# Order of scores, values and exponentials in a causal attention loop, and the PSUM bank that holds the value sums

## The chip, the cores and the metric

The kernel runs on 1 core of a Trainium2 chip. The time is device microseconds of one execution. TensorE (PE) multiplies and transposes into PSUM, which has 8 banks of 128 partitions x 512 fp32; VectorE (DVE) and ScalarE (ACT) read PSUM and write SBUF; GpSimd (POOL) works on SBUF alone here; SyncE (SP) issues the DMAs. Each engine runs its own instructions in the order in which they were issued and waits at an instruction until what it needs is there.

## What is computed

One encoder-decoder layer in fp32. Encoder: 2 sequences of 77 tokens, D = 512, 16 heads of 32, self attention with a relative bias, feed-forward of 2048. Decoder: 2 sequences of 2048 tokens: causal self attention with a relative bias, cross attention to the encoder's output, feed-forward. What this change touches is the decoder's causal self attention:

```
def _mha(xq, xkv, w_in, b_in, w_out, b_out, bias):
    wq, wk, wv = jnp.split(w_in, 3, axis=0)
    ...
    scores = jnp.einsum('bhqd,bhkd->bhqk', q, k) / jnp.sqrt(jnp.asarray(hd, xq.dtype))
    scores = scores + bias[None]
    attn = jax.nn.softmax(scores, axis=-1)
    out = jnp.einsum('bhqk,bhkd->bhqd', attn, v)
    out = out.transpose(0, 2, 1, 3).reshape(Bq, Tq, D)
    return out @ w_out.T + b_out
...
sb = _rel_bias(dec_rel_self, Tt, Tt) + causal[None]
yn = _ln(y, dec_n1_s, dec_n1_b)
y = y + _mha(yn, yn, dec_sa_in_w, dec_sa_in_b, dec_sa_out_w, dec_sa_out_b, sb)
```

## The kernel before

**Tiling.** The 2048 queries of a batch b (0, 1) are four blocks m (0 to 3) of 512, each four tiles t (0 to 3) of 128. The 16 heads are four groups g of four heads r. A *unit* is one (b, m, g, t): 128 queries, four heads; there are 128. It sees i + 1 = 4m + t + 1 blocks of 128 keys: 1 to 4 in block 0, 5 to 8 in block 1, 9 to 12 in block 2, 13 to 16 in block 3. `pieces` cuts these into pieces of at most four key blocks: 9 is 4 + 3 + 2, 10 is 4 + 4 + 2, 11 is 4 + 4 + 3, 12 is 4 + 4 + 4, 16 four times 4.

**Steps of a unit.** `scores` (one call for each piece): four matmuls, one for each head, with 32 rows of the array each, into four banks (L374); DVE copies each head's bank to the buffer `pp` and keeps its maximum (L383; the last two key blocks go with the bias through L390); after the last piece L399 makes the negative maximum `nm`, and the four exponentials (L404, ACT, one for each head, over the whole width of the unit) are put into the list `late_exps`. `exps(k)` issues the first k of them. `turn`: transposes the probabilities of up to two pieces, one bank for each key block with its four heads (a *load*, L424), and copies each bank to `pts`, the first half of the loads on ACT (L430), the rest on DVE (L428). `values`: for each key block four matmuls, 32 columns of the array each, add v times the transposed probabilities into bank 7 (L441), which gathers the four units t of a group in its four quarters; after the last one the whole bank is copied to `oT` (L447). Later the sums of the exponentials divide `oT` on POOL (L469), and `out_job` (L251) projects it and adds the residual, which `residual` loads on SP and adds to the bias on POOL (L266).

**Two buffers.** `pp` holds the scores of two units, so while unit n is turned, unit n + 1 is complete or nearly so, and `may_score` lets a piece of unit n + 2 in as soon as unit n's turn has read that part.

**The main loop** takes the pieces two at a time. Each round is a *visit*: all exponentials still missing for this unit, `turn` (in block 0 another order of loads), at the unit's last visit `slot(n + 1)` (the *jobs* of that unit: projections of q, k and v, the output projection, norms, weight sums), a score piece, one or two exponentials, `values`, further score pieces. Within `turn` one exponential is issued behind the fourth load (or the last, if there are fewer) and one behind the last load. A unit of block 1 is one visit, of blocks 2 and 3 two.

**Banks.** `bank()` hands out banks 0 to 6 in turn (`count`), bank 7 is for the value sums. PE waits before it writes a bank until the engine that read it last is done. Behind the attention loop the feed-forward half takes over with banks 0 to 3 for `bank()`.

The lines of the main loop that are moved:

```
            if may_score():
                score_next()
            if ends:
                for f in behind[n + 1]:
                    f()
            exps((0, 2, 1, 1)[units[n][1]])
            for p in pair:
                values(*p)
            while may_score() and (len(pair) > 1 or units[n][1] == 0):
                score_next()
```

## Time and profile before

| what | value |
|---|---|
| median of 3 runs | 2781.49 us (2779.92 to 2781.69) |
| the profiled execution's own time | 2781.64 us |
| its span | 2779.9 us |
| granted PE clock | 0.998 |
| ACT and DVE busy | 1436.6 and 1888.2 us |
| HBM traffic | 129 GB/s over the span |

The attention loop, with the encoder and the first block's cross attention woven in, is the first 1705 us; its blocks begin at 29, 165, 381 and 616 us (batch 0) and 888, 1024, 1215 and 1448 us (batch 1). Then comes cross attention and feed-forward. A row of the timeline is: start, length, engine, line, operation, what it writes and reads, shape, number of records, and in brackets the engine's idle time before it and what ended it. A score matmul or a values matmul leaves two records in the trace, a transpose one: "x32" at L424 is eight loads, "x8" at L374 a piece (four heads), "x64" at L441 the values of eight key blocks. PEld are the weight loads, which run beside PE.

### The profile page before, as it was taken

How to read it: one execution, taken by the hardware profiler on the slowest of the kernel's cores; microseconds unless marked ns; L12 is line 12 of the kernel's file. 1: busy time of each engine (PE TensorE's matmuls, PEld its weight loads, DVE VectorE, ACT ScalarE, POOL GpSimd, SP SyncE). 2: the span in 40 equal slices, each digit the busy share in tenths (PEclk: the TensorE clock that was granted, in tenths of full speed). 3: DMA queues.
4: the chain of work that ended last, by engine and by line, in shares of the span. 5: the costliest groups of instructions: out<-in, count | busy, mean ns of one | idle time of the engine just before them, and what ended most of it. 6: DMA issues, size and time to landing. Idle time of an engine off the chain costs nothing. (4 is left out here: it accounts for less than half of the span.)

```text
span 2779.9 us, 66840 instructions
## 1 busy us (share of the span) xinstructions
PE 2750.5 (99%) x26294; PEld 2130.5 (77%) x26294; DVE 1888.2 (68%) x5420; ACT 1436.6 (52%) x2753; POOL 915.8 (33%) x777
## 2 busy tenths in 40 slices
PE   9999999999999999999999999999999999999998
PEld 5577776677666566676677667898989898989898
DVE  5776587788887578687788885555555646464645
ACT  3444466656666556666656665444444444444431
POOL 1501134400100412212200002364646474646456
PEclk9999999999999999999999999999999999999999
DMA  8433345411112521233211014574757565646465
GB/s 224 141 102 111 102 124 166 128 55 47 35 52 62 139 74 55 89 100 104 96 55 40 25 32 141 186 233 156 228 159 234 176 223 163 222 161 224 147 225 182
DMA packets 282251, 362.45 MB, mean 130 GB/s; under 512 B 39072, under 2 KB 156624, under 8 KB 281810
## 3 DMA queue, kind: packets, MB, share of 16 engines
q1 hardware_dynamic: 281938, 358.18, 41.0%
q8 instruction: 208, 3.41, 0.5%
q14 instruction: 105, 0.86, 0.1%
HBM read 314.49 MB, written 43.59 MB: 129 GB/s over the span
## 5 line engine op out<-in xcount | busy, mean ns | idle before, releaser
L404 ACT ACTIVATE pp<-pp,nm 128x128 f32<-128x128 f32 (+15 forms) x512 | 612.1, 1203 | 146.6 <-DVE nm L399 142.1
L383 DVE TENSOR_SCALAR_CACHE_REDUCE pp<-psum 128x512 f32<-128x512 f32 (+3 forms) x1024 | 559.3, 591 | 59.4 <-PE psum L374 57.7
L424 PEld LDWEIGHTS psum<-ident,pp 128*128 128x128 f32 x4352 | 473.1, 141 | 112.8 <-DVE pp L383 56.0
L424 PE MATMUL psum<-ident,pp 128*128 128x128 f32 x4352 | 535.8, 277 | 10.1 <-DVE mx L390 3.3
L430 ACT COPY pts<-psum 128x512 f32<-128x512 f32 (+3 forms) x592 | 300.6, 576 | 470.4 <-PE psum L424 339.0
L428 DVE COPY pts<-psum 128x512 f32<-128x512 f32 (+2 forms) x544 | 330.0, 660 | 66.2 <-PE psum L424 65.7
L374 PE MATMUL psum<-kT,q 32*128 32x512 f32 (+3 forms) x2560 | 357.0, 574 | 4.5 <-ACT nT L310 2.1
L441 PEld LDWEIGHTS psum<-pts,vv 128*32 128x32 f32 x8704 | 225.6, 110 | 123.3 <-issue 115.5
L1524 PE MATMUL psum<-pp 128*128 128x128 f32 x2560 | 304.5, 276 | 1.9 <-POOL pp L936 1.6
L1524 PEld LDWEIGHTS psum<-pp 128*128 128x128 f32 x2560 | 296.3, 192 | 8.6 <-issue 2.8
L441 PE MATMUL psum<-pts,vv 128*32 128x128 f32 x8704 | 278.2, 275 | 0.7 <-ACT pts L430 0.5
L936 POOL TENSOR_TENSOR pp<-pp 128x512 f32<-128x512 f32 x159 | 212.7, 1354 | 126.3 <-DMA pp<-in_dec_ff_wT_dram 66.3
L1495 PE MATMUL psum<-vv,pp 128*128 128x256 f32 x1024 | 236.2, 381 | 0.0
L374 PEld LDWEIGHTS psum<-kT,q 32*128 32x128 f32 x2560 | 121.3, 183 | 123.2 <-issue 80.2
L1495 PEld LDWEIGHTS psum<-vv,pp 128*128 128x128 f32 x1024 | 190.3, 190 | 25.8 <-issue 0.5
L390 DVE CUSTOM_DVE_ANT_0 pp<-psum,bias 128x256 f32<-128x256 f32 (+1 forms) x512 | 196.3, 412 | 14.7 <-PE psum L374 14.5
L1508 DVE TENSOR_TENSOR kT<-kT,psum 128x512 f32<-128x512 f32 x96 | 65.8, 686 | 191.1 <-PE psum L1495 190.9
L266 POOL TENSOR_TENSOR xr<-xr,row_dec_sa_out_b 128x512 f32<-128x512 f32 x30 | 38.2, 1276 | 417.9 <-DMA xr<-in_x_dram 313.1
L1495 PE MATMUL psum<-nT,pp 128*128 128x256 f32 x768 | 174.1, 380 | 0.0
L1511 ACT ACTIVATE kT<-kT,vecs 128x256 f32<-128x256 f32 x192 | 87.0, 501 | 156.7 <-DVE kT L1508 156.0
L1495 PEld LDWEIGHTS psum<-nT,pp 128*128 128x128 f32 x768 | 144.2, 190 | 20.3 <-issue 1.6
L469 POOL TENSOR_TENSOR oT<-rirows,oT 128x512 f32<-128x512 f32 x30 | 38.3, 1275 | 364.4 <-DMA rirows<-rec 327.9
(242 smaller groups left out, 3882.8 us busy)
## 6 DMA issues: line engine op xcount, KB each, us to landing
pp<-w_d SPq DMA_DIRECT2D x520, 256.0 KB
pp<-in_dec_ff_wT_dram SPq DMA_DIRECT2D x112, 256.0 KB
wqk<-in_dec_sa_in_wT_dram SPq DMA_DIRECT2D x76, 256.0 KB
bias<-tzg SPq DMA_DIRECT2D x128, 128.0 KB
pp<-wo_d SPq DMA_DIRECT2D x56, 256.0 KB
vv<-in_enc_ff_wT_dram SPq DMA_DIRECT2D x8, 1024.0 KB
xr<-in_x_dram SPq DMA_DIRECT2D x32, 256.0 KB
vv<-y SPq DMA_DIRECT2D x32, 256.0 KB
```

The lines of the kernel that those rows point to most:

```text
L374: nc.tensor.matmul(banks[r][:, : kn * P], q[rows4(r), ts(t, P)], kT[rows4(r), g, k0 * P : (k0 + kn) * P], start=True, stop=True,)
L383: nc.vector.tensor_scalar(p[:, k0 : k0 + far], s[:, :far], 1.0, None, ALU.mult, ALU.max, accum_out=st["mx"][:, r, c : c + 1],)
L390: nc.vector.tensor_tensor_reduce(p[:, k0 + far : i + 1], s[:, far:kn], near[:, 2 - (kn - far) :], 1.0, LOWEST, ALU.add, ALU.max, accum_out ...
L404: nc.scalar.activation(p, p, AF.Exp, bias=nm, accum_out=to)
L424: nc.tensor.transpose(pt[:, ts(x, P)], state[n]["p"][r][:, k], ident)
L428: nc.vector.tensor_copy(pts[:, : len(load), :], pt[:, :w])
L430: nc.scalar.copy(pts[:, : len(load), :], pt[:, :w])
L441: nc.tensor.matmul(ot[rows4(r), t, :], vv[:, k, ts(g * HC + r, HD)], got.pop((n, k, r)), start=(k == 0), stop=(k == i),)
L936: engine.tensor_tensor(out, a, b, ALU.subtract)
L1495: nc.tensor.matmul(mm[:, ts(f, TOK)], a[:, c, ts(f, P)], b[:, c, :], start=fresh and f == 0 and c == 0, stop=c == 1, skip_group_check=True,)
L1511: nc.scalar.activation(dst[:, e, :], src[:, e, :], AF.Relu, bias=vec("dec_ff1_b", f + e))
L1524: nc.tensor.matmul(psum[:, bank_i, ts(col, P)], lhs[:, c, :], w[:, c, :], start=fresh and k in (0, 3) and c == 0, stop=c == 3, skip_group_ ...
```

## The change

1. `bank()` takes the bank that has been handed out longest ago from a ring of all eight. `values` takes the oldest bank out of the ring and puts it back, as the newest, behind the copy of its sums.
2. `values` is called once for a visit's pair. In block 0 one bank gathers a group's four units as before and is copied whole on ACT. In the other blocks each visit has a bank of its own: the first visit's sums are copied to `oT` on ACT (128x128), the second visit's are added to them on DVE. In the first tile of the third group the sums stay in the bank over both visits (so `oT` is written after its last reader).
3. In blocks 1 to 3, a visit with two pieces scores up to two pieces ahead of `values`; what may still be scored comes behind as before.
4. The one or two exponentials behind `turn` are issued ahead of the score calls. In a turn of eight loads the exponential that was behind the fourth load is behind the eighth; in block 3 the one that followed the turn is left to the next place.
5. In a turn of eight loads (blocks 1 to 3) DVE copies loads 4 and 6 (counted from 0), ACT the other six.
6. The output projection of blocks 0 to 2 is one unit earlier, with its residual.

In the built program PE has the same instructions before and after, in another order. ACT's copies of whole banks to `pts` go from 544 to 688, DVE's from 496 to 352; ACT's copies of 128x128 to `oT` from 56 to 152; DVE's 24 copies of whole banks to `oT` are gone, its additions of 128x128 to `oT` go from 56 to 116 (56 of each of these two belong to the feed-forward half).

```diff
@@ -174,13 +174,13 @@
         oT_all = ac.tile([P, 6, TB * P], F32, name="oT")
         bo = ac.tile([P, D], F32, name="row_dec_sa_out_b")
         psum = ps.tile([P, 8, 512], F32, name="psum")
-        count = {"bank": 0, "banks": 7, "pts": 0, "oT": 0, "mm": 0}
+        count = {"pts": 0, "oT": 0, "mm": 0}
+        ring = list(range(8))
 
         def bank():
 
-            i = count["bank"] % count["banks"]
-            count["bank"] += 1
-            return psum[:, i, :]
+            ring.append(ring.pop(0))
+            return psum[:, ring[-1], :]
 
         def in_turn(what, tile):
             i = count[what] % tile.shape[1]
@@ -424,27 +424,47 @@
                     nc.tensor.transpose(pt[:, ts(x, P)], state[n]["p"][r][:, k], ident)
                     got[n, k, r] = pts[:, x, :]
                 w = len(load) * P
-                if o % 2 if first else o >= (len(loads) + 1) // 2:
+                if o % 2 if first else o in (4, 6) if len(loads) == 8 else o >= (len(loads) + 1) // 2:
                     nc.vector.tensor_copy(pts[:, : len(load), :], pt[:, :w])
                 else:
                     nc.scalar.copy(pts[:, : len(load), :], pt[:, :w])
-                if not first and o == min(3, len(loads) - 1):
+                if not first and o == (7 if len(loads) == 8 else min(3, len(loads) - 1)):
                     exps(1)
-            exps(HC if first else 1)
-
-        def values(n, k0, kn):
+            exps(HC if first else 0 if units[pieces[0][0]][1] == NMB - 1 else 1)
+
+        sums_held = {}
+
+        def values(pair):
+            n, k0, _ = pair[0]
             b, m, g, t = units[n]
             i = m * TB + t
-            for k in range(k0, k0 + kn):
-                ot = psum[:, 7, :].rearrange("p (t q) -> p t q", q=P)
+            k1 = pair[-1][1] + pair[-1][2]
+            whole = m == 0
+            key = (b, m, g) if whole else n
+            begun = key in sums_held
+            if not begun:
+                sums_held[key] = ring.pop(0)
+            v = sums_held[key]
+            ot = psum[:, v, ts(t, P)] if whole else psum[:, v, :P]
+            keep = t < TB - 1 if whole else (g, t) == (2, 0) and k1 <= i
+            for k in range(k0, k1):
                 for r in range(HC):
                     nc.tensor.matmul(
-                        ot[rows4(r), t, :], vv[:, k, ts(g * HC + r, HD)], got.pop((n, k, r)),
-                        start=(k == 0), stop=(k == i),
+                        ot[rows4(r)], vv[:, k, ts(g * HC + r, HD)], got.pop((n, k, r)),
+                        start=k == k0 and (whole or not begun), stop=k == k1 - 1 and (whole or not keep),
                     )
-                if t == TB - 1 and k == i:
-                    o = ots[b, m, g] = in_turn("oT", oT_all)
-                    (nc.vector.tensor_copy if m else nc.scalar.copy)(o, psum[:, 7, :])
+            if keep:
+                return
+            if (b, m, g) not in ots:
+                ots[b, m, g] = in_turn("oT", oT_all)
+            o = ots[b, m, g]
+            if whole:
+                nc.scalar.copy(o, psum[:, v, :])
+            elif k0 == 0 or begun:
+                nc.scalar.copy(o[:, ts(t, P)], ot)
+            else:
+                nc.vector.tensor_tensor(o[:, ts(t, P)], ot, o[:, ts(t, P)], ALU.add)
+            ring.append(sums_held.pop(key))
 
         ri_of = [const.tile([P, RB], F32, name=f"ri{i}") for i in range(2)]
         for t in ri_of:
@@ -1094,9 +1114,10 @@
                 jobs[NU + 5].append(fold_job())
             for t in range(TB):
                 end = x == len(blocks) - 1
-                jobs[u + NU + (2 if end else 7) + t].append(out_job(b, m, t))
+                out_at = u + NU + (2 if end else 7 if m == NMB - 1 else 6) + t
+                jobs[out_at].append(out_job(b, m, t))
                 if not end:
-                    light[u + NU + 6 + t].append(lambda b=b, m=m, t=t: residual(b, m, t))
+                    (light if x else late)[out_at - 1].append(lambda b=b, m=m, t=t: residual(b, m, t))
                 elif t < 2:
                     light[u + NU - 1].append(lambda b=b, m=m, t=t: residual(b, m, t))
                 if x:
@@ -1743,14 +1764,14 @@
             turned_to[n] = pair[-1][1] + pair[-1][2]
             if ends and n + 1 < end:
                 slot(n + 1)
-            if may_score():
-                score_next()
+            exps((0, 2, 1, 1)[units[n][1]])
+            for _ in range(2 if len(pair) > 1 and units[n][1] else 1):
+                if may_score():
+                    score_next()
             if ends:
                 for f in behind[n + 1]:
                     f()
-            exps((0, 2, 1, 1)[units[n][1]])
-            for p in pair:
-                values(*p)
+            values(pair)
             while may_score() and (len(pair) > 1 or units[n][1] == 0):
                 score_next()
             i += len(pair)
@@ -1759,7 +1780,8 @@
         for t in (2, 3):
             residual_load(*blocks[-1], t, pts_all[:, 2 * t - 3, :])
         late_loads()
-        count.update(bank=0, banks=4)
+        assert len(ring) == 8
+        ring[:] = range(4)
         side = cross(1)
         slot(end)
         for s in range(4):
```

## The prediction

> **What bounds the kernel now.** I read the page's busy table first.
>
> ```profile
> span 2779.9 us, 66840 instructions
> PE 2750.5 (99%) x26294; PEld 2130.5 (77%) x26294; DVE 1888.2 (68%) x5420; ACT 1436.6 (52%) x2753; POOL 915.8 (33%) x777
> ```
>
> PE bounds it, but matmuls are pipelined, so a waiting PE still shows as busy. What PE really needs is read from the start of one group to the start of the next, in the timeline of a visit where nothing waits (here the first visit of a unit of block 3, batch 0):
>
> ```profile
> 739.26 3.71 PE L424 MATMUL psum<-ident,pp 128*128 128x128 f32 x32
> 739.95 2.06 ACT L430 COPY pts<-psum 128x512 f32<-128x512 f32 x4 [4.48 <-PE psum L424]
> 742.90 1.14 PE L374 MATMUL psum<-kT,q 32*128 32x512 f32 x8
> 743.97 1.95 PE L441 MATMUL psum<-pts,vv 128*32 128x128 f32 x64
> 744.10 0.68 DVE L383 TENSOR_SCALAR_CACHE_REDUCE pp<-psum 128x512 f32<-128x512 f32 x1
> 745.86 1.14 PE L374 MATMUL psum<-kT,q 32*128 32x512 f32 x8
> 746.93 3.77 PE L424 MATMUL psum<-ident,pp 128*128 128x128 f32 x32
> ```
>
> Eight loads of transposes take 742.90 - 739.26 = 3.64 us, a score piece of four blocks 1.07, the values 1.89, the second piece 1.07: 7.67 in all. A group's busy time is its share plus a tail of 0.07 (1.14 against 1.07, 3.71 against 3.64). Next, the groups by shape, to see how much of PE's time is waiting:
>
> ```profile
> L424 PE MATMUL psum<-ident,pp 128*128 128x128 f32 x4352 | 535.8, 277 | 10.1 <-DVE mx L390 3.3 <-ACT pp L404 2.8 <-ACT nT L310 1.4
> L374 PE MATMUL psum<-kT,q 32*128 32x512 f32 x1600 | 255.4, 637 | 0.0
> L374 PE MATMUL psum<-kT,q 32*128 32x384 f32 x448 | 52.8, 533 | 0.0
> L374 PE MATMUL psum<-kT,q 32*128 32x256 f32 x448 | 45.3, 423 | 1.7 <-DVE pp L383 1.4 <-DVE kT L1043 0.3
> ```
>
> A score piece is 8 records, so 200, 56 and 56 pieces; clean they are busy 1.14, 0.93 (row at 454.83 below) and, taking the same step of 0.21 per block, 0.71 us: 228 + 52 + 40 = 320. The rows say 353.5, so some 33 us are waits for banks and about 2 more are idle. Transposes: 136 times 3.71 is 505; 192 turns instead of 136 full ones add about 56 x 0.15 = 8 of starts and tails; the row says 535.8, so 23 are waits, and 10 more idle. PE therefore waits about 70 us at these two lines in a chain that is otherwise matmul after matmul. That is the room. It is not spread evenly; by block of batch 0 (blocks 1, 2, 3) the scores take
>
> ```profile
> 165.00:381.20 216.20, 37.04 (x273) 13.16 (x272) 1.00 0.33 108
> 381.20:616.10 234.90, 61.69 (x392) 22.05 (x392) 0.99 0.41 123
> 616.10:887.90 271.80, 63.61 (x472) 19.39 (x472) 1.00 0.13 38
> ```
>
> (stretch, its length, PE busy, PEld busy, clock, DMA). Block 2 has 32 + 8 + 8 pieces, 36.5 + 7.4 + 5.7 = 49.6 clean, and shows 61.7: 12 us of waits. Block 1 (34 pieces, about 33.6 clean) has 3.4. Block 3 (59 pieces at 1.06) has 1. The engines in blocks 2 and 3:
>
> ```profile
> 381.20:616.10 234.90, 233.95 (x2600) 164.72 (x2600) 187.87 (x605) 145.14 (x235) 72.97 (x61) 0.99 0.41 123
> 616.10:887.90 271.80, 271.41 (x3399) 191.62 (x3393) 225.45 (x709) 180.54 (x267) 20.71 (x16) 1.00 0.13 38
> ```
>
> (PE, PEld, DVE, ACT, POOL busy.) DVE is at 80 to 83%, ACT at 62 to 66%: neither is the bound, but PE waits when one is late for a bank.
>
> **Part 1: two pieces side by side.** The pair price is in one place of the trace where it happens already, a piece of three blocks ahead of one of two; a lone piece of three stands in the next fence but one, with its values behind it.
>
> ```profile
> 366.25 2.26 PE L374 MATMUL psum<-kT,q 32*128 32x384 f32 x16
> ...
> 367.00 1.51 PE L374 MATMUL psum<-kT,q 32*128 32x256 f32 x8
> ```
>
> The second piece starts 0.75 after the first; alone, a piece of three takes 455.69 - 454.83 = 0.86. So 0.11 us are saved for each pair. In the built program 113 pieces stand directly ahead of another, 17 before: 96 x 0.11 = **10.6 us** if PE is the bound in each of these visits, nothing in those where ACT is (Part 3). The Trainium skill, "TensorEngine Tiling (Array Packing)", Key Properties, says that a change of tiling mode drains TensorE, and "TensorE: Matmul & The Clock Gate", Single matmul latency, puts a drain at about 175 ns; one change less per visit would by these pages be an estimated 16.8 us instead. The row prices the same thing here and I go by it.
>
> **Part 2: exponentials behind the copies.** Before, an exponential is put into ACT's queue behind the score call, so it waits for those scores' maximum, and the next turn's copies queue behind it:
>
> ```profile
> 423.78 1.26 ACT L404 ACTIVATE pp<-pp,nm 128x1152 f32<-128x1152 f32 x1 [3.97 <-DVE nm L399]
> 425.03 2.02 ACT L430 COPY pts<-psum 128x512 f32<-128x512 f32 x4
> 426.43 1.81 PE L374 MATMUL psum<-kT,q 32*128 32x512 f32 x8
> ...
> 441.32 2.16 PE L374 MATMUL psum<-kT,q 32*128 32x512 f32 x8
> ```
>
> The copies come 1.4 us late and the piece takes 1.81 instead of 1.14: 0.7 lost. Six visits of block 2 in each batch are of this kind: three t = 3 units, and three t = 0 units, where it is 1.0 (441.32). Issued ahead of the score call, the exponentials left in the queue are those whose maximum is long known, and this wait goes: 2 x (3 x 0.7 + 3 x 1.0) = **10 us** (0 to 10).
>
> **Part 3: the eighth bank, and what is late next.** In block 2 the unit t = 1 goes: eight loads, a piece of three, values, then two pieces of four.
>
> ```profile
> 454.83 0.93 PE L374 MATMUL psum<-kT,q 32*128 32x384 f32 x8
> 455.69 1.69 PEld L441 LDWEIGHTS psum<-pts,vv 128*32 128x32 f32 x64 [0.55 <-issue]
> 457.57 3.03 PE L374 MATMUL psum<-kT,q 32*128 32x512 f32 x16
> 458.57 1.47 ACT L404 ACTIVATE pp<-pp,nm 128x1408 f32<-128x1408 f32 x1 [4.58 <-DVE nm L399]
> ...
> 460.54 1.09 PE L424 MATMUL psum<-ident,pp 128*128 128x128 f32 x8
> 461.27 0.58 ACT L430 COPY pts<-psum 128x512 f32<-128x512 f32 x1 [1.14 <-DVE pp L383]
> 461.76 1.47 ACT L404 ACTIVATE pp<-pp,nm 128x1408 f32<-128x1408 f32 x1
> 464.67 1.46 ACT L404 ACTIVATE pp<-pp,nm 128x1408 f32<-128x1408 f32 x1
> 466.28 5.05 PE L424 MATMUL psum<-ident,pp 128*128 128x128 f32 x29 [0.95 <-ACT pp L404]
> ```
>
> The two pieces need eight banks of a ring of seven: 460.54 - 457.57 = 2.97 where 1.93 would do, 1.04 lost, four times a batch. After, the order is three, four, values, four; the wait for a bank shrinks to about 0.3. But the gain is given back: the piece of three completes the next unit's scores, and its exponentials now find no place in this visit (the one that ran at 458.57 is asked for before the scores exist). All four run in the short visit behind: 8.41 us from the long visit's start to the short one's (3.64 + 0.75 + 1.07 + 1.88 + 1.07), 0.73 to ACT's copy, 0.49 to the first exponential, 3 x 1.46 to the last, 1.61 from there until PE goes on (466.28 - 464.67): 15.6. Before, the long visit takes 3.64 + 0.86 + 1.88 + 2.97 = 9.35 and the short one, with a job of 3.45, 0.93 + 3.45 + 1.07 + 0.57 = 6.02: 15.4. So nothing is won in these four units of a batch, and 0.2 to 0.5 lost in each. In the rows above the short visit has no job, and PE waits; blocks 1 and 2 have their output projections one unit earlier after the change, so this unit gets a job and the next t = 1 unit loses its own: the wait moves. I take **+3 us** for both batches (-8 if the chain stays hidden, to +10).
>
> With a projection go its residual's load on SP and the addition on POOL, one unit earlier too, behind that unit's weight sums:
>
> ```profile
> 447.86 2.06 POOL L936 TENSOR_TENSOR kT<-pp,kT 128x384 f32<-128x384 f32 x2
> 453.04 1.27 POOL L266 TENSOR_TENSOR xr<-xr,row_dec_sa_out_b 128x512 f32<-128x512 f32 x1 [3.12 <-DMA xr<-in_x_dram]
> ```
>
> POOL is free at 449.9, and the moved projection's matmuls end near 465: 15 us cover it, so 0.
>
> **Part 4: copies moved to ACT, sums kept in SBUF.** Of eight copies six now run on ACT (four before): 144 copies leave DVE at 0.62 each and cost ACT 0.51 (2.06 for four, row at 739.95). 24 whole-bank sums on DVE become 96 of 128x128 on ACT and 60 additions on DVE, bounded by
>
> ```profile
> L1532 ACT COPY oT<-psum 128x128 f32<-128x128 f32 x56 | 14.9, 267 | 239.2 <-PE psum L1524 239.2
> L1540 DVE TENSOR_TENSOR oT<-psum,oT 128x128 f32<-128x128 f32 x56 | 15.7, 281 | 0.0
> L404 ACT ACTIVATE pp<-pp,nm 128x2048 f32<-128x2048 f32 x32 | 64.0, 2000 | 4.9 <-DVE nm L399 4.9
> ```
>
> DVE: -89 - 16 + 17 = -88 us; ACT: +74 + 26 = +100. Block 3, eight loads, four + four, eight: PE 3.64 + 0.96 + 1.07 + 1.89 = 7.56. ACT: its last copy ends about 4.5 after the turn starts (transposes 3.64, then 0.25 and 0.58), two exponentials of at most 2.0, a sum copy 0.27: 8.8, and the next turn's first copy is due at 7.56 + 0.69 = 8.25. So ACT starts up to 0.55 late, and its copies 5 and 7 have 0.6 to spare as copies 4 and 6 are DVE's. The values' bank is that of the first piece's first head: DVE starts on it 1.2 after the piece does (744.10 - 742.90) and frees it 0.7 later, 1.9, when the values are due at 2.03. DVE's other seven evictions end 6.2 after it and the next turn reaches their banks 0.2 to 0.4 behind. It fits, narrowly. What doesn't fit are the second visits without a job at the end of batch 1, where the last exponential is behind the copies: some 0.5 each, and about 3 in the last three visits, where no score piece covers it. Against that stand block 3's own waits. I take **-3 us** for block 3 (-8 to +6).
>
> **Part 5: block 1.** Four exponentials a visit as before, in no new place among ACT's copies but for visits of eight loads. The 3.4 us of waits at the scores in each batch, and by length about as much of the transposes' 33, are for banks and for late jobs; the eighth bank and the output job one unit earlier shorten them. I take **-6** (0 to -13). Block 0 keeps its order: 0. The feed-forward half, which starts here, is not touched:
>
> ```profile
> 1705.13 7.11 PE psum L1495 x32
> ```
>
> **The sum.** -10.6 - 10 + 3 - 3 - 6 = -26.6. The profiled execution took 2781.64 (span 2779.9), the median of the runs is 2781.49, so both give 2755.
>
> **Rivals.**
> (a) All waits go: the room of 70 us less block 0's share (about 20), and the pairs: -50 - 10.6, 2721; a middle way to it is 2736. For it: ACT is at 66% at most. Against it: the chain of four exponentials in Part 3.
> (b) Taken back: the pairs and Part 2 are real, but the exponentials, now later everywhere, hold the next turn: Part 3 at +10, block 3 at +6, and block 1 without gain: 2781.6 - 20.6 + 16 = 2777 to 2782.
> (c) Slower: in block 3 ACT starts a turn's copies more than 0.6 us late. Then the second piece waits for the bank of copy 7, the values behind it, and ACT's 8.8 us set the visit instead of PE's 7.56. That is 64 visits; at 0.6 each +38 instead of -3, 2796. It decides from 0.05 us beyond what I count, which speaks for it; against it, the second visits have jobs of 1.7 to 3.5 us that let ACT catch up. The Trainium skill, "TensorEngine Tiling (Array Packing)", Gotcha 1: PSUM Pressure, warns of it: row tiles need a bank each, and two pieces take all eight.
>
> **How the numbers follow.** Forecast 0.55, (a) 0.17, (b) 0.10, (c) 0.18. The forecast's own range is 2742 to 2768. To hold 8 in 10 the range takes in the middle of (a) and all of (b): 2729 to 2782, leaving out (c) and the far end of (a). A change below 0.2% (5.6 us) can't be told from none here: faster 0.73, same 0.09, slower 0.18.
>
> **What would show it.** Pairs: the second piece of four starts 0.96 behind the first. Part 2: the first copy of a turn 0.7 behind its transposes in every visit of block 2. Part 3: four exponentials of 1408 in a row in the short visit, and PE waiting for the last. Part 4: DVE busy in block 3 near 200, ACT near 200; a piece of four taking over 1.3 behind another says (c). The forecast is wrong if the attention half (to 1705 us) ends after 1702 or before 1660.

## The result and the profile after

| what | before | after |
|---|---|---|
| median of 6 runs | 2781.78 us (2779.92 to 2782.24) | 2770.24 us (2768.68 to 2771.65) |
| ratio to before | 1 | 0.9959, 95% interval 0.9947 to 0.9972 |
| span of the profiled execution | 2779.9 us | 2769.9 us |
| granted clock of the profiled execution | 0.998 | 0.995 |
| block 0 (batch 0, batch 1) | 136.2, 135.9 | 137.5, 136.6 |
| block 1 (in the same order) | 216.2, 191.1 | 214.2, 193.1 |
| block 2 | 235.0, 233.4 | 229.8, 230.7 |
| block 3 | 271.7, 256.9 | 268.1, 256.5 |
| feed-forward half, to the end of the span | 1074.8 | 1074.8 |

The change gains 11.5 us where 26.6 were forecast: the right sign, inside the range, less than half the size. A stage here runs from the first transpose of its first turn to that of the next stage, and the time of a visit below is counted in the same way, from turn to turn. Everything happened in the attention half, which now ends at 1695.1 instead of 1705.1. By block (both batches together) the time changes by -7.9 in block 2, -4.0 in block 3, 0 in block 1 and +1.9 in block 0. The forecast, with its 96 new pairs of pieces spread over the blocks as the program has them (28, 14 and 54, at 0.11), was -9.1 in block 1, -8.5 in block 2 and -8.9 in block 3. What is missing is all of block 1 and half of block 3; block 2 came within 0.6 us, though not by the parts that were added up for it. The prediction's own sign of being wrong, an attention half that ends outside 1660 to 1702, did not come; only the split by blocks shows which parts failed.

The line of busy times on the page after, and then the windows of blocks 2 and 3 of batch 0 (stretch, its length, busy time of PE, PEld, DVE, ACT and POOL, granted clock, DMA):

```profile
PE 2724.6 (98%) x26294; PEld 2154.4 (78%) x26294; DVE 1807.0 (65%) x5312; ACT 1538.8 (56%) x2993; POOL 915.6 (33%) x777
```

```profile
380.30:610.10 229.80, 224.25 (x2601) 162.44 (x2600) 175.99 (x592) 160.25 (x274) 73.06 (x61) 0.99 0.42 126
610.10:878.20 268.10, 265.89 (x3397) 199.16 (x3393) 204.17 (x680) 207.31 (x324) 20.73 (x16) 1.00 0.13 40
```

DVE falls by 81 us and ACT rises by 102, as worked out (-88, +100), and in block 3 both stand near 200. So the work went where it was meant to go. The groups by shape:

```profile
L374 PE MATMUL psum<-kT,q 32*128 32x512 f32 x1600 | 228.4, 624 | 0.6 <-ACT nT L310 0.5
L424 PE MATMUL psum<-ident,pp 128*128 128x128 f32 x4352 | 536.4, 278 | 20.2 <-ACT pp L404 13.5 <-DVE mx L390 3.0 <-ACT nT L310 1.4
L452 PE MATMUL psum<-pts,vv 128*32 128x128 f32 x8704 | 279.5, 276 | 6.7 <-DVE pp L383 4.2 <-ACT pts L430 0.2
```

The score pieces of 512 are busy 27 us less (255.4 before, 228.4 now). That is not free of waits, although 228 was worked out as clean for pieces one by one: two pieces of four side by side are busy 2.00 when nothing waits (next fence), not 2 x 1.14, and the changed kernel has 52 such pairs where the one before has 12. By that estimate the clean figure is 213 now and was 225, and the waits in these pieces fell from some 31 us to some 15. The idle time ahead of the transposes doubled, from 10.1 to 20.2, and most of it is now for exponentials (L404), 13.5 against 2.8. The values, which waited for next to nothing (0.7), now wait 6.7, most of it for DVE. These are the two new waits that the rest of this document follows. A visit of block 3 in which nothing waits:

```profile
733.74 3.71 PE L424 MATMUL psum<-ident,pp 128*128 128x128 f32 x32
737.38 2.00 PE L374 MATMUL psum<-kT,q 32*128 32x512 f32 x16
738.54 0.69 DVE L383 TENSOR_SCALAR_CACHE_REDUCE pp<-psum 128x512 f32<-128x512 f32 x1 [0.79 <-PE psum L374]
739.31 1.96 PE L452 MATMUL psum<-pts,vv 128*32 128x128 f32 x64
741.19 0.98 PE L424 MATMUL psum<-ident,pp 128*128 128x128 f32 x7
```

It takes 741.19 - 733.74 = 7.45 us (7.67 before). The pair takes 739.31 - 737.38 = 1.93 for 2 x 1.07 alone: 0.21 saved, twice the 0.11 that the prediction took from an unequal pair. DVE empties the first head 1.16 + 0.69 = 1.85 after the pair begins, and the values come at 1.93: the fit is as narrow as it was worked out. Where the second piece is narrower than four blocks it isn't a fit, as in block 1:

```profile
204.23 1.36 PE L374 MATMUL psum<-kT,q 32*128 32x384 f32 x16
...
205.18 0.56 DVE L383 TENSOR_SCALAR_CACHE_REDUCE pp<-psum 128x384 f32<-128x384 f32 x1 [0.46 <-PE psum L374]
205.80 1.74 PE L452 MATMUL psum<-pts,vv 128*32 128x128 f32 x56 [0.21 <-DVE pp L383]
```

Three + two blocks are through at 205.59; DVE leaves the first head's bank, which is the values' bank, just before 205.8, and PE stands still for 0.21.

Last, the unit t = 1 of block 2 that has no output projection in its short visit any more (Part 3's wait, moved as the prediction said):

```profile
515.92 1.47 ACT L404 ACTIVATE pp<-pp,nm 128x1408 f32<-128x1408 f32 x1
517.39 1.46 ACT L404 ACTIVATE pp<-pp,nm 128x1408 f32<-128x1408 f32 x1
518.84 1.49 ACT L310 ACTIVATE nT<-psum,vecs 128x128 f32<-128x128 f32 x4
518.94 0.44 PE L424 MATMUL psum<-ident,pp 128*128 128x128 f32 x2
520.21 1.47 ACT L404 ACTIVATE pp<-pp,nm 128x1408 f32<-128x1408 f32 x1
521.66 1.47 ACT L404 ACTIVATE pp<-pp,nm 128x1408 f32<-128x1408 f32 x1
521.83 0.33 PE L424 MATMUL psum<-ident,pp 128*128 128x128 f32 x1 [2.45 <-ACT pp L404]
523.28 4.73 PE L424 MATMUL psum<-ident,pp 128*128 128x128 f32 x29 [1.12 <-ACT pp L404]
```

Four exponentials of the next unit (t = 2, 1408 wide) are asked for in this short visit, with another job's copies (L310) among them. Two of them have run when the next turn starts at 518.94; PE waits for the other two. Then the 29 transposes take 4.73 us, where 29 take 3.38 elsewhere: TensorE ran at a lower granted clock:

```profile
523.00:525.00 2.00, 1.72 (x8) 0.50 1.03 287
525.00:527.00 2.00, 2.00 (x16) 0.73 1.04 289
```

(stretch, length, PE busy, granted clock, DMA.) The wait costs more than its own length. With both, the unit and the visit behind it (505.89 to 531.73) take 25.85 us against 23.1 for its fellows with a job.

The clock takes a share of the whole result that no part of the prediction has. By the clock records of the two traces, TensorE ran at half clock in the attention half for 6.8 us before (two stretches) and for 23.9 us after (five): in block 0, in a visit of block 1 of batch 1, behind the waiting unit of either batch, and in the last visits. Set against the same visits at full clock in other runs, the added stretches cost some 6.5 us (an estimate: 1.2, 1.6, 2.0 and 1.7). The one in block 1:

```profile
1137.00:1139.00 2.00, 2.00 (x41) 1.62 (x34) 1.75 (x11) 0.56 (x3) 1.92 (x3) 0.51 0.00 0
```

(stretch, length, busy time of PE, PEld, DVE, ACT and POOL, granted clock, DMA.) Which of these stretches come with the change and which are chance is taken up in the last section.

### The profile page after: what moved, and what is told of

It is laid out like the page before. It is cut to its first block, busy times and chain, and to the rows that moved or that the text cites. A ratio compares the mean times of both kernels' runs of the same rounds, so it can differ in the third digit from the quotient of the medians.

```text
span 2769.9 us, 67113 instructions
## 1 busy us (share of the span) xinstructions
PE 2724.6 (98%) x26294; PEld 2154.4 (78%) x26294; DVE 1807.0 (65%) x5312; ACT 1538.8 (56%) x2993; POOL 915.6 (33%) x777
## 3 DMA queue, kind: packets, MB, share of 16 engines
q8 instruction: 208, 3.41, 0.5%
## 4 chain that ended last, share of the span: by engine, by line
PE 89%; DVE 4%; ACT 3%; issue 1%; POOL 1%; DMA 1%; SPq 0%; POOLq 0%; DVEq 0%; ACTq 0%
PE psum L424 17%; PE psum L1516 14%; PE psum L1545 12%; PE psum L374 9%; PE psum L452 8%; PE psum L1038 4%; PE psum L251 4%; PE psum L215 4%; PE psum L1676 3%; PE psum L1633 3%; ACT pp L404 3%; DVE pp L383 2%; PE psum L860 2%; PE psum L830 1%; PE psum L868 1%
## 5 line engine op out<-in xcount | busy, mean ns | idle before, releaser
L404 ACT ACTIVATE pp<-pp,nm 128x128 f32<-128x128 f32 (+15 forms) x512 | 611.8, 1201 | 34.5 <-DVE nm L399 34.0
L424 PE MATMUL psum<-ident,pp 128*128 128x128 f32 x4352 | 536.4, 278 | 20.2 <-ACT pp L404 13.5
L430 ACT COPY pts<-psum 128x512 f32<-128x512 f32 (+2 forms) x736 | 386.5, 580 | 298.9 <-PE psum L424 258.0
L374 PE MATMUL psum<-kT,q 32*128 32x512 f32 (+3 forms) x2560 | 321.6, 559 | 4.6 <-ACT nT L310 2.6
L452 PEld LDWEIGHTS psum<-pts,vv 128*32 128x32 f32 x8704 | 226.7, 110 | 122.5 <-DVE pp L383 67.5
L428 DVE COPY pts<-psum 128x512 f32<-128x512 f32 (+3 forms) x400 | 249.5, 654 | 106.6 <-PE psum L424 104.4
L374 PEld LDWEIGHTS psum<-kT,q 32*128 32x128 f32 x2560 | 138.4, 183 | 125.6 <-issue 53.6
L1529 DVE TENSOR_TENSOR kT<-kT,psum 128x512 f32<-128x512 f32 x96 | 65.8, 686 | 191.1 <-PE psum L1516 190.9
```

The lines of the kernel that those rows point to most:

```text
L374: nc.tensor.matmul(banks[r][:, : kn * P], q[rows4(r), ts(t, P)], kT[rows4(r), g, k0 * P : (k0 + kn) * P], start=True, stop=True,)
L404: nc.scalar.activation(p, p, AF.Exp, bias=nm, accum_out=to)
L424: nc.tensor.transpose(pt[:, ts(x, P)], state[n]["p"][r][:, k], ident)
L428: nc.vector.tensor_copy(pts[:, : len(load), :], pt[:, :w])
L430: nc.scalar.copy(pts[:, : len(load), :], pt[:, :w])
L452: nc.tensor.matmul(ot[rows4(r)], vv[:, k, ts(g * HC + r, HD)], got.pop((n, k, r)), start=k == k0 and (whole or not begun), stop=k == k1 - ...
```

## Experiments

All are edits of the changed kernel (2770.24 us); the ratios are to the kernel before.

**The moved projections.** First, the output projections back where they were:

```
-out_at = u + NU + (2 if end else 7 if m == NMB - 1 else 6) + t
+out_at = u + NU + (2 if end else 7) + t
```

> The changed kernel with its output projections of blocks 0 to 2 one unit later again, where they stood before the change. In the changed kernel the t = 1 unit of block 2 that has no projection in its short visit (from 505.9 to 531.7 us) takes 25.85 us, and its three fellows, which have a job there, take 23.1. My theory: the short visit without a job is what costs, wherever it lies, so here the wait moves to the unit that begins at 448.6 (23.1 -> 25.9), the other one falls to 23.1, and the same in batch 1: the time stays at 2770, within 2 us. The rival: moving the projections is itself what lost the 2.2 and 3.2 us that these units grew by, and the time falls by 5 to 7 us, to 2764.

Measured: 2771.98 us, ratio to before 0.9966 (0.9953 to 0.9978). The wait moved to the unit from 448 on, where PE waits and then runs 29 transposes in 5.05 us at 465.64. What costs is the short visit without a job, wherever it lies. Then it can be removed: there are five ends of units for four projections, and two of the five are short t = 1 visits.

```
+out_at = u + NU + (2 + t if end else 7 + t if m == NMB - 1 else (6, 7, 9, 10)[t])
```

> The changed kernel with the four output projections of a block at the ends of the sixth, seventh, ninth and tenth unit instead of the sixth to ninth, so that every t = 1 unit of block 2 has a job in its short visit; the slot left empty is that of a t = 3 unit. If the short visit without a job is what costs (my theory), block 2 loses no unit of 25.85 or 26.81 us: these fall to 23.1, the stalls of 5.5 and 6.4 us go, and the time falls by 6 to 11 us, to 2759 to 2764. The rival: the wait belongs to the queue of exponentials as a whole and comes back in the t = 3 unit that now has no job (its short visit grows by over 2 us against the 4.0 that it loses of work): then 2770, within 2 us.

Measured: 2759.55 us, 0.9918 (0.9904 to 0.9931), 10.7 below the changed kernel. Block 2 takes 225.0 us in both batches (229.8 and 230.7). The place that lost its wait:

```profile
514.98 1.48 ACT L404 ACTIVATE pp<-pp,nm 128x1408 f32<-128x1408 f32 x1
516.43 1.47 ACT L404 ACTIVATE pp<-pp,nm 128x1408 f32<-128x1408 f32 x1
518.05 3.38 PE L424 MATMUL psum<-ident,pp 128*128 128x128 f32 x29 [1.12 <-ACT pp L404]
```

PE still waits 1.12 for the last exponential, but not for the one before, and the clock stays at 1.00: 29 transposes in 3.38. The same edit lost 4 us in block 3 of batch 0: a visit of eight loads without its projection waited 1.87 us for ACT's copies (L310), which stood behind an exponential, and TensorE then ran at half clock for 6.8 us. Later versions leave block 2's own projections, which run there, as the change has them.

**The pairs.** One score piece ahead of the values again, everything else as changed:

```
-for _ in range(2 if len(pair) > 1 and units[n][1] else 1):
+for _ in range(1):
```

> The changed kernel with one score piece ahead of a visit's values again and the other behind them; eight banks, copies and exponentials as in the changed kernel. My theory: side by side a pair of equal width saves 0.21 us and one of unequal width 0.11 us on TensorE, of which the values' wait for a bank takes back 9 us in all; one piece ahead, the values take a bank long free, so the time rises by 3 to 8 us only, to 2773 to 2778. The rival (Part 1 of the prediction, each pair worth 0.11 us with nothing taken back): 2781. A second rival: one piece ahead has the next unit's scores complete later and the exponentials hold its transposes: over 2785.

Measured: 2761.47 us, 0.9934 (0.9921 to 0.9946): 8.8 us *faster*. No theory had it. The pairs, the first part of the sum, cost time. By stage the difference was -4.1 and -5.5 in block 1, +1.6 and +0.9 in block 2, -0.6 and -1.2 in block 3. Two stretches at half clock in the changed kernel's profile are in this: 1.6 of the 5.5 us (at 1137: the two visits that it falls in take 11.17 + 14.53, and 10.34 + 13.74 in the version with the exponentials behind the score calls), and 1.7 in the last visits of block 3. Without them the pairs cost 7.9 in block 1 and about nothing in block 3. A visit of block 1 with one piece ahead, and the same visit of the changed kernel:

```profile
349.14 1.14 PE L374 MATMUL psum<-kT,q 32*128 32x512 f32 x8
350.21 1.52 PE L452 MATMUL psum<-pts,vv 128*32 128x128 f32 x48
351.66 1.14 PE L374 MATMUL psum<-kT,q 32*128 32x512 f32 x8
352.73 0.44 PE L424 MATMUL psum<-ident,pp 128*128 128x128 f32 x2
```

```profile
352.57 2.64 PE L374 MATMUL psum<-kT,q 32*128 32x512 f32 x16
352.75 1.29 DVE L1063 TENSOR_TENSOR kT<-psum,kT 128x512 f32<-128x512 f32 x2 [1.10 <-PE psum L1038]
353.96 0.68 DVE L383 TENSOR_SCALAR_CACHE_REDUCE pp<-psum 128x512 f32<-128x512 f32 x1
...
355.14 1.52 PE L452 MATMUL psum<-pts,vv 128*32 128x128 f32 x48
356.59 0.66 PE L424 MATMUL psum<-ident,pp 128*128 128x128 f32 x4
```

From the first piece to the next turn: 352.73 - 349.14 = 3.59 with the pieces apart, 356.59 - 352.57 = 4.02 side by side. In block 1 every visit has a job ahead of its score pieces. DVE empties the job's banks first (L1063, to 354.0) and comes late to the pair; the pair's second piece and the values wait for it. With values between the pieces DVE has 1.45 us of TensorE's time in which it catches up.

The same in block 1 alone:

```
+for _ in range(2 if len(pair) > 1 and units[n][1] > 1 else 1):
```

> The changed kernel with two score pieces ahead of the values in blocks 2 and 3 only; in block 1 one piece goes ahead again. With one piece ahead everywhere the time fell by 9 us, and stage by stage it was block 1 that fell, by 4.1 us in batch 0 and 5.5 in batch 1, while blocks 2 and 3 and the rest came within 2 us of where they were. My theory: in block 1 the second piece leaves VectorE behind, and the values and the job after them wait for banks; so this kernel takes 2759 to 2763. The rival: one piece ahead gains through blocks 2 and 3 as well, by way of what reaches the next block late: then only half of it or less is seen, 2766 to 2770.

Measured: 2762.29 us, 0.9935 (0.9923 to 0.9948); block 1 took 210.1 and 187.6, as with one piece ahead everywhere. The cost of the pairs is block 1's.

**The values' bank.** Two attempts to take that wait away and keep the pairs. In the first the values are summed in the free quarter of a narrow second piece's bank:

```
+narrow_bank[0] = banks[-1][:, 3 * P :] if kn < 4 else None
 ...
+beside = None if whole or begun or keep else narrow_bank[0]
+ot = beside
```

> The changed kernel, but where the score piece ahead of a visit's values is narrower than four blocks, the values are summed in the free last quarter of that piece's fourth bank instead of the oldest bank of the ring. My theory: in the changed kernel the values behind a pair of pieces of four + two, three + two or four + three wait 0.31, 0.18 and 0.09 us until VectorE has emptied the first head of the first piece, whose bank they take, some 9 us in all with the mixed ones; here that wait is gone (four + two + values: 1.91 -> about 1.6 us), and the time falls by 5 to 9 us, to 2761 to 2765. The rival: the values are held by TensorE's own change between kinds of matmuls, not by the bank: same pieces, same time, 2770 within 2 us.

Measured: 3028.15 us, 1.0884 (1.0869 to 1.0899). Neither theory. The waits of the values' weight loads (engine, line, waited for: us in all, times, longest):

```profile
PEld psum L459 <- DVE mx L392: 183.4, 62, 4.8
PEld psum L459 <- DVE pp L385: 80.7, 62, 4.5
```

The values now wait until DVE has emptied that bank, the last of the eight, although they write other columns. The Trainium skill, "PSUM — Partial Sum Buffer", PSUM bank collisions raise a hardware error, says that the compiler orders any two instructions of different engines on the same bank and partitions, whatever the columns; the trace agrees, with waits of up to 4.8 us. The granted clock fell to 0.965 with it. This run says nothing on the question it was made for.

In the second, of two pieces of one unit the narrower goes first, and its banks are free earlier:

```
+scores(n, k1, kn1, False)
+scores(n, k0, kn, True)
```

> The changed kernel, but where the two score pieces ahead of a visit's values are of one unit and the second is the narrower one (four + two, four + three, three + two), the narrow piece is issued first; its maxima are still reduced behind both. The values take the bank of the first head of the first piece; a narrow piece leaves it earlier. My theory: the waits of 0.31, 0.18 and 0.09 us of the values behind these pairs are for that bank and go (four + two + values in 1.91 us becomes two + four + values in 1.6 to 1.8), and the time falls by 2 to 8 us, to 2762 to 2768. The rival: the values wait for TensorE's own switch from row tiles to column tiles behind a short piece, whatever the order: nothing is gained, 2770 within 2 us.

Measured: 2779.60 us, 1.0000 (0.9991 to 1.0008). The wait for the bank did go, and the time rose by 9:

```profile
L374 PE MATMUL psum<-kT,q 32*128 32x512 f32 (+3 forms) x2560 | 330.2, 561 | 4.2 <-ACT nT L310 2.6 <-ACT kT L231 0.7 <-DVE pp L383 0.5
L424 PE MATMUL psum<-ident,pp 128*128 128x128 f32 x4352 | 542.0, 280 | 26.5 <-ACT pp L404 18.8 <-DVE mx L390 3.0 <-ACT nT L310 1.4
L452 PE MATMUL psum<-pts,vv 128*32 128x128 f32 x8704 | 278.0, 275 | 0.4 <-ACT pts L430 0.2
```

The values are idle for 0.4 (6.7), but the score pieces are busy 330.2 (321.6) and the transposes wait 18.8 for exponentials (13.5). The first turn of block 2 in each batch alone lost 6 us, with a chain of four exponentials and the clock at 0.50 behind it. So the wait was for the bank, as held. What it stands for, by these sums, is that DVE is behind: the 6.3 us that the values no longer wait are met again at the score pieces (+8.6).

**The ring.** The sums in a bank of their own, the ring seven banks:

```
-ring = list(range(8))
+ring = list(range(7))
-sums_held[key] = ring.pop(0)
+sums_held[key] = 7
```

> The changed kernel with the values' sums in a bank of their own and a ring of seven, as before the change: the two score pieces side by side share seven banks. My theory: the fourth head of the second piece waits until the first head of the first piece has been emptied, 1.9 us after the pair's start instead of 0.96, while the values no longer wait: some 0.6 to 1.0 us for each of the 96 pairs, slower by 50 to 90 us, 2820 to 2860. The rival: the bank that the values wait for is the whole cost of the ring, and with one of their own the time falls by up to 9 us, to 2761.

Measured: 2846.65 us, 1.0239 (1.0225 to 1.0253). Pairs without the eighth bank lose 76 us:

```profile
780.72 1.60 PE L374 MATMUL psum<-kT,q 32*128 32x512 f32 x14
782.63 0.69 PE L374 MATMUL psum<-kT,q 32*128 32x256 f32 x2 [0.31 <-DVE pp L383]
```

The last head of the second piece starts 782.63 - 780.72 = 1.91 after the first piece, as worked out.

**The exponentials.** Behind the score calls again:

```
-exps((0, 2, 1, 1)[units[n][1]])
 for _ in range(2 if len(pair) > 1 and units[n][1] else 1):
 ...
+exps((0, 2, 1, 1)[units[n][1]])
 values(pair)
```

> The changed kernel with a visit's exponentials issued behind its score calls again (and behind the jobs), ahead of the values, so that the first of them may be one of the unit whose scores have just been completed. My theory (Part 2 of the prediction): in block 2 the six visits of each batch of the kinds t = 3 and t = 0 get back the wait of 0.9 and 1.0 us that the change took away, the t = 1 units win back about 0.5 each since one exponential leaves the chain of four, and the time rises by 5 to 12 us, to 2775 to 2782. The rival: with two pieces ahead of the values the order among the exponentials no longer matters, and the time stays at 2770 within 2 us.

Measured: 2766.74 us (2766.22 to 2771.69), 0.9952 (0.9939 to 0.9964). Undoing Part 2 cost nothing that the time shows; the two intervals overlap. In the profile the waits came back as foretold, 0.8 in t = 3 and 0.54 in t = 0 visits:

```profile
421.75 2.78 PE L374 MATMUL psum<-kT,q 32*128 32x512 f32 x16
```

(the same pair takes 2.00 in the changed kernel). But three t = 2 visits of each batch win 0.76, since one exponential of the chain runs a visit earlier, and block 3's first visit wins 0.77. Block 2 changes by +1.7 and -0.3; the two differ by where half clock fell behind the waiting unit. The 3.5 us by which the median is lower are not explained by the edit: in the profiled run 2.8 lie in block 0, which it does not touch, and 1.6 in the stretch at half clock of block 1 (the last section shows why these vary).

Inside the turn, as before the change:

```
-if not first and o == (7 if len(loads) == 8 else min(3, len(loads) - 1)):
+if not first and o == min(3, len(loads) - 1):
-exps(HC if first else 0 if units[pieces[0][0]][1] == NMB - 1 else 1)
+exps(HC if first else 1)
```

> The changed kernel with the exponentials inside a turn at the fourth load again (not the eighth), and one at its end in block 3 too, so three a visit there. My theory: the two last of ACT's six copies of eight then start behind an exponential of 1.2 to 2.0 us, the second score piece waits for their banks, and every visit of eight loads in blocks 2 and 3 loses about 1 us; the second visits of block 3 without a job win back 0.3 each and the tail about 3.6. In all slower by 40 to 90 us, 2810 to 2860. The rival: ACT, at 66% of the attention half at most, has room, and only the winnings show: 2763 to 2767.

Measured: 2804.54 us, 1.0089 (1.0075 to 1.0103), less than expected, with the mechanism that was named:

```profile
745.84 1.72 ACT L404 ACTIVATE pp<-pp,nm 128x1664 f32<-128x1664 f32 x1
746.87 2.91 PE L374 MATMUL psum<-kT,q 32*128 32x512 f32 x16
747.51 1.09 ACT L430 COPY pts<-psum 128x512 f32<-128x512 f32 x2
```

ACT's last two copies stand behind an exponential, and the pair takes 2.91 instead of 2.00. Block 3 lost 15.8 and 13.2.

**The copies.** Four and four again:

```
-o in (4, 6) if len(loads) == 8 else o >= (len(loads) + 1) // 2
+o >= (len(loads) + 1) // 2
```

> The changed kernel with ACT copying the first four of a turn's eight loads and VectorE the last four, as before the change, instead of six and two. My theory: VectorE, with eight evictions (5 us) and four copies (2.5 us) in a visit of 7.46 us, has no room left in block 3; its copies start behind the evictions of the visit before and the second score piece waits for their banks: slower by 2 to 12 us, 2772 to 2782, all of it in blocks 2 and 3. The rival: ACT with six copies and two exponentials is the tighter one, and its relief shows: 2762 to 2768.

Measured: 2793.86 us, 1.0048 (1.0034 to 1.0061), more than expected. DVE's four copies in a row come too late for the pair:

```profile
743.79 2.48 DVE L428 COPY pts<-psum 128x512 f32<-128x512 f32 x4 [0.95 <-PE psum L424]
744.99 2.46 PE L374 MATMUL psum<-kT,q 32*128 32x512 f32 x16
```

A clean visit of block 3 takes 7.91, one behind a late DVE up to 8.8. The three visits ahead of the last one of batch 1, where DVE has no scores left, are faster by 3 us (18.3 instead of 21.4), 1.7 of it by the clock.

**Together.** The runs' gains in one version: pairs in blocks 2 and 3 only, the projections spread (blocks 0 and 1), an exponential that found none ahead of the score calls tried again behind them, and another share of copies and exponentials in the last two units.

```
+out_at = u + NU + (2 + t if end else 7 + t if m == NMB - 1 else 6 + t if m == 2 else (6, 7, 9, 10)[t])
 ...
+k = 2 if n >= end - 2 else (0, 2, 1, 1)[units[n][1]]
+left = max(0, k - len(late_exps))
+exps(k)
+for _ in range(2 if len(pair) > 1 and units[n][1] > 1 else 1):
 ...
+exps(left)
```

> A version put together from what the runs showed: the changed kernel with two pieces ahead in blocks 2 and 3 only (-9.6), the projections of blocks 0 and 1 at the sixth, seventh, ninth and tenth unit (-10 in block 2; those of block 2 stay where the change put them), an exponential that finds none to issue ahead of the score calls issued behind them (-0.76 in three t = 2 visits of each batch, -4), and in the last two units copies shared half and half between the engines and three exponentials a visit (-4 of the tail's 4.3). If these add up, 2743, within 4 us. The rival: they share one wait, that of the exponentials, and do not add up: 2750 or more.

Measured: 2748.64 us, 0.9882 (0.9869 to 0.9896). Block 1 gave what was expected (210.1, 186.1), block 2 took 226.7 rather than about 223: the second try of the exponentials does just what undoing Part 2 did, and the t = 0 visit behind the projection-free one takes 1.66 more (7.60 for 5.94). The three visits ahead of the last one took 21.5, no gain.

```
+wide = not ends and [p[2] for p in stream[at[0] : at[0] + 2]] == [4, 4]
+for _ in range(2 if len(pair) > 1 and (units[n][1] == 2 or units[n][1] == 3 and wide) else 1):
```

> As the version before it, but in block 3 two pieces ahead only in a unit's first visit and only where both are four wide, since there the pair wins 0.21 us on TensorE (7.67 -> 7.46) and no wait of the values was seen, while the visits 82 to 85 were 2.0 us shorter with one piece ahead. My theory: 1 to 4 us below the version before it. The rival: what a pair wins in a first visit comes back in the second (10.68 -> 10.88 in t = 3), so both take the same time within 1 us.

Measured: 2745.85 us, 0.9873 (0.9860 to 0.9887), an interval that overlaps the one before, so the stages have to tell. In block 3 pairs of four + four in a unit's first visit win, the others lose (267.1 -> 264.4, 255.9 -> 254.3).

Next, without the second try, and with the copies of the last two units alone changed (second half on DVE):

> The version of 2745.9 us with two of its edits taken back or replaced: a visit's exponentials are issued ahead of the score calls alone, as in the changed kernel (no second try behind them), and in the last two units only the copies differ from the changed kernel (the second half on VectorE), not the number of exponentials. My theory: with the projections spread, no t = 1 unit waits any longer, and Part 2's own worth in block 2 can be seen: 226.7 -> 225.0 us a batch, less 0.8 at the start of block 3; the tail (visits 189 to 191) takes 18.3 instead of 22.1 us. In all 2739 to 2743. The rival: issuing exponentials ahead of the score calls wins nothing in block 2 here either, as it did not in the changed kernel, and only the tail shows: 2742 to 2746.

Measured: 2741.28 us, 0.9856 (0.9842 to 0.9869), the lowest median, 29 us below the changed kernel (its interval overlaps those of its neighbours). Block 2 takes 225.3 in both batches: with the waiting unit out of the way, Part 2 is worth 1.4 us a batch. The three visits ahead of the last one took 20.5 instead of the 18.3 expected; in the next version, alike there, they took 18.8 (the last section shows the 1.7 between them).

```
+for _ in range(2 if len(pair) > 1 and units[n][1] == 3 and wide else 1):
```

> The version before it with one score piece ahead of the values in block 2 too, so that two go ahead only in block 3's first visits, where both are four wide. My theory: in block 2 a pair is worth what it saves, 1 to 2 us a batch (231.5 us with one piece ahead against 229.8 and 230.7 with two, all with the unit that waits), so this one is slower by 2 to 4 us. The rival: that difference lay in the waiting unit alone, and without it both are the same within 1 us. A second rival (Part 1 of the prediction): the pairs of block 2 are a third of the 96 and worth 0.11 us each, 3.5 us.

Measured: 2743.02 us, 0.9863 (0.9850 to 0.9877); the two intervals overlap. By stage block 2 takes 226.7 and 226.8, so its pairs are worth 1.4 and 1.5 us, 2.9 in all, as the theory had it. (They are 14 of the 96, not a third.) The medians are only 1.7 apart.

## Why the prediction was half right

**Part 1, the pairs (-10.6): the step that failed.** It stands as "96 x 0.11 = 10.6 us if PE is the bound in each of these visits, nothing in those where ACT is". The saving itself is larger than taken, 0.21 where both pieces are four wide. (Part 3 of the prediction reckons with 1.93 us for two such pieces, which is this 0.21; Parts 1 and 4, with 0.96 + 1.07 = 2.03, do not.) But the sentence knows two outcomes, gain and nothing, and looks for the other bound at ACT. It is DVE: two pieces are eight evictions (copies out of a score bank) in a row, and the values wait for the first. Part 4 looked at this wait for one case alone, four + four in block 3 ("It fits, narrowly"), where it holds. In block 1, with a narrow second piece or a job's evictions ahead, it doesn't. Where 10.6 us were to be gained, undoing the pairs gained 8.8. Of these, 3.3 are the two stretches at half clock, by the profiled executions; the pairs themselves lose 7.9 in block 1, about nothing in block 3, and gain 2.5 in block 2 (2.9 without the waiting unit). That the pairs set off the stretch at 1137 is not shown; other versions with the same pairs there do not have it.

**Part 2, the exponentials (-10): held in its places, given back in others.** The waits of 0.7 and 1.0 went (t = 3 visits 8.34 -> 7.46, t = 0 visits 6.97 -> 5.94), 5.8 us a batch. But undoing it changes block 2 by +1.7 and -0.3 only. The exponentials are one queue: what one visit issues earlier, a later one has to issue, and the t = 2 visits and block 3's first visit wait 0.8 each for it. The prediction counted the giving back in the t = 1 units, and there at a smaller price. Its net worth is 1.4 a batch, measured where no other wait covers it.

**Part 3 (+3): right in kind, mis-sized.** The units t = 1 gained and lost as described: the wait for a bank shrank from 1.04 to 0.4, and the unit without a job moved. Together these units, each with the visit behind it, lost 6 us in the two batches instead of 3; about 2 of the 6 are more half clock. In the one without a job PE waited 2.45 + 1.12 us for the last two exponentials where before it waited 0.95 for one, and the 29 transposes behind it took 4.73 instead of 3.38. That second term was in the quoted rows (29 transposes in 5.05 at 466.28) and was passed over. And "the wait moves" was taken as given; that one projection moved by one unit more removes it, the prediction did not see.

**Part 4 (-3): the copies and sums as worked out,** DVE -81, ACT +102, the fit of four + four to 0.1 us, and the three visits ahead of the last one 18.7 -> 21.4 (about 3 forecast). That last agreement is in part luck: 1.7 of the 2.7 us are half clock (29 transposes in 5.05 at 1682.67, behind the same waits 3.38 with one piece ahead), so without it they would take 19.7. Without the pairs block 3 gains 5.8, more than the 3 of this part; with them it gains 4.0, where 8.9 were forecast. The pairs that lose are those in second visits and those of unequal width: without them, in the versions put together above, the block takes 2.7 and 1.6 us less. That is Part 1's step again; 1.7 is the half clock of the last visits.

**Part 5 (-6): right, and hidden.** Without the pairs block 1 falls from 216.2 and 191.1 to 210.1 and 187.6, -9.5 by the unrounded times, for the eighth bank and the earlier projections, inside the 0 to -13 given. The pairs took back 7.9 of it and half clock 1.6, which is why block 1 shows nothing.

**The rivals.** (b) came nearest by its mechanism: real savings, taken back by exponentials that hold the next turn; but DVE, which it does not name, took a share too, and its time, 2777 to 2782, was missed by 7 us. (c) did not come: ACT is on time in block 3 unless an exponential is put among its copies, which makes it true at once (2804.5). Rival (a), that all waits go, is 2721; the best version here, at 2741, is two thirds of the way there.

**The sum** was made as if the parts added. They share two resources, DVE's evictions and the queue of exponentials, and each was priced as if the others left these alone. No part had the clock, although the rows of the prediction show it once (5.05 us for 29 transposes).

## What to carry to other kernels

- Work put side by side on the bounding engine sends its consumers a burst; price the step for the engine that has to empty the banks, with the job that it may still be busy with, in every kind of visit and not only in the cleanest.
- A wait on the bounding engine can cost more than its own length. Compare visits at the same granted clock before an edit gets the credit; some 6.5 of the 15 us missing here, by estimate, went there.
- When a queue is reordered, follow the whole queue for one period: a gain at one place is a gain only if the instructions that moved have idle time where they land.
- A wait that merely moves with a piece of work is worth a look at where that work could go instead; here one line that spreads four projections over five places was worth nearly as much as the whole change.

## What the runs showed of the hardware

**A short wait can halve TensorE's clock, or not, by chance.** Each stretch at half clock in the attention half of these traces lasts 3.41 us or twice that. In block 0 PE waits 2.10 us for ACT near 112 us, before the change and after. In the changed kernel's profile (stretch, length, PE busy, granted clock, DMA):

```profile
112.00:114.00 2.00, 0.21 (x3) 0.76 0.03 8
114.00:116.00 2.00, 2.00 (x31) 0.50 0.00 0
```

and in that of the version with the exponentials behind the score calls, which issues the same instructions in block 0:

```profile
112.00:114.00 2.00, 0.62 (x14) 1.00 0.01 4
114.00:116.00 2.00, 2.00 (x37) 1.00 0.00 0
```

Block 0 takes 137.5 us in the one and 134.6 in the other; most of the "loss" of block 0 in the table above is this. The last two versions, alike in their last units, show it on one wait of 1.65 us, first the fastest version, then the one with a single piece ahead in block 2:

```profile
1652.32 5.05 PE L424 MATMUL psum<-ident,pp 128*128 128x128 f32 x29 [1.65 <-ACT pp L404]
```

```profile
1655.26 3.38 PE L424 MATMUL psum<-ident,pp 128*128 128x128 f32 x29 [1.65 <-ACT pp L404]
```

In the kernel before, one execution shows both. Its unit of batch 0 at 466.28, quoted in the prediction, takes 5.05 behind a wait of 0.95; the same unit of batch 1 does not:

```profile
1299.90 3.38 PE L424 MATMUL psum<-ident,pp 128*128 128x128 f32 x29 [0.95 <-ACT pp L404]
```

So waits of 0.95 and 1.65 us cost 1.67 more, and one of 2.10 cost 2.9 more, in some places and nothing more in others. Behind the unit without a job, where PE waits 1.41 to 2.51 us and in most cases about 1 us again, half clock followed in both batches of the changed kernel and of seven versions that keep this unit: 16 of 16. There the stretches are a cost of the waiting unit; elsewhere they came in some executions and not in others. The Trainium skill, "TensorE: Matmul & The Clock Gate", What's actually happening, says that the clock is halved after an idle window of about 3.4 us and that this window runs freely, so that the moment depends on its phase. The traces agree with the halving (0.50) and with the chance; no single wait shown ahead of such a stretch here was as long as 3.4 us.

**Sums in another quarter of a bank's columns still wait for the engine that reads the bank** (up to 4.8 us, in the version with the sums beside a narrow piece).
